# A two-layer graph network on one core: 15 of 1563 gathered chunks fetched row by row by the SyncE queue, with joint register loads and a third buffer for z

## Chip, core and metric

The kernel runs on one core of one Trainium2 chip. A core has TensorE (PE, matrix products, with a separate weight load, PEld), VectorE (DVE), ScalarE (ACT), GpSimd (POOL) and SyncE (SP, which here only issues transfers). The engines run their own instruction streams in order and wait for one another through semaphores. The metric is the device time of one execution in microseconds (us), the median over several runs.

## What is computed

Two message-passing layers over the same graph, with 12,500 nodes of 64 features, 200,000 edges sorted by destination, and 8 edge types. Each layer's result is added to its input and normalised. Cut to what matters:

```python
# layer 1: a message of each edge, summed by destination
all_feat = concatenate([x[dst], x[src], edge_attr, u_per_node[dst]])
msg = relu(all_feat @ W1 + b1)
agg = segment_sum(msg, dst)
x = layernorm(x + relu(concatenate([x, agg, u_per_node]) @ W2 + b2))

# layer 2: attention over the edges of a destination, by edge type
Z = einsum('ni,rio->nro', x, fc_weight)        # (node, type, 64)
z_s, z_d = Z[src, etype], Z[dst, etype]
e = relu(sum(concatenate([z_s, z_d]) * attn_weight[etype], axis=1))
ex = exp(e - segment_max(e, dst)[dst])
alpha = ex / segment_sum(ex, dst)[dst]
x = layernorm(x + segment_sum(alpha * z_s, dst))
```

In the second layer one row of Z is needed for each edge: the row of its source node and its type.

## The kernel before

**Tiling.** Edges come in chunks of 128 (`EC`), one edge per partition. Four chunks make a run (`KS`), which shares one window of 96 (`W`) destinations. Two runs make a group of eight chunks (`K`). There are 1563 chunks and `NG` = 196 groups; the last has three chunks.

**Layer 1** (some 0 to 2600 us) gathers rows of a table from DRAM for each chunk (L95), forms the messages, and sums them by one-hot matrix products. `finish0` turns a tile of 125 nodes into the first layer's output and into that tile's rows of Z, which go through a tile `z` (L477 to L481) to the DRAM table `z_tab`. That has one row for each node and type, with `C` = 65 values (260 bytes): the 64 of Z and the source's share of the score. A smaller table `d_tab` holds the destinations' shares.

**Layer 2** (some 2640 to 5340 us) is `sum1`, one Python generator per group. Its pieces, in order:

- The loads. SP: `row` (L501, four buffers), two registers with the windows' first nodes (L330), and two window loads into `dw` (L600, four buffers) whose DRAM addresses are in those registers. POOL: eight indirect transfers (L95), one for each chunk, each of 128 rows of `z_tab` into `zg` (five buffers).
- `ps_row`, `off`, `ohT`, `pq` (L609 to L618): the destinations' shares, by PE and ACT.
- `oh` (L355): the one-hot matrix, on DVE, in one instruction of 0.95 us.
- `er`, `ed`, `e`, score, `oe` to `t` (L624 to L646): scores and their maximum by destination, on DVE. Score is the first that reads `zg`.
- Transposes (L652), then register loads on DVE and ACT, then `m` (L657) and `rows` (L659).
- `most`, `d`, `top` (L667 to L669): the running maximum of each destination, kept in SBUF, its columns addressed by registers.
- `column`, `mq`, `pm` (L677, L428 to L431, L684): the maximum is brought back to each edge. `pm` is eight small matmuls.
- `em` (L688, L689), the exponentials (L690, L692), and `wz` (L694): eight ACT instructions that scale the rows of `zg`. They are the last that read `zg`, and free it.
- `sums` (L698), sixteen PE matmuls, and `acc` (L702, L703).

`finish1` turns 125 nodes of `acc` into the layer's output (from iteration 90, `FIRST`), with a load of `xn` on SP. `scale1` normalises every fourth iteration, and SP stores four tiles of `out` (L744).

**Order.** The loop runs over `i` from -3 to `NG` - 3. An iteration advances several groups by a piece each, in an order written out by hand in calls of `group()` and `node()`, which the compiler keeps on each engine. The loads of group i+3 come first. SP and POOL have nothing else in their streams, so they run ahead of the other engines as far as the buffers allow. SP issues in order: what waits for a buffer holds back all that is behind it. A transfer with its address in a register is three instructions on SP: register arithmetic, a move and the DMA itself.

**Register loads.** `wins_load` loads each window's number by an instruction of its own, for each of the engines that need it; `group` and `node` are the calls of `next` on the generators.

Of the kernel before, what the change touches and what calls it, by code (L numbers as in the profile page):

```python
# [45 lines left out]
S = 2  # L46
# [7 lines left out]
W = 96  # L54
NWIN = (N + W - 1) // W
GX = 5
FIRST = 90
NSL = NG - FIRST
LAST = 6
# [8 lines left out]


@with_exitstack  # L70
def gnn_kernel(ctx: ExitStack, tc, x, xT, xP, src, dstp, dst, et, eaT, u, W1, b1, W2, b2, fc, aw, out):
    nc = tc.nc
    consts = ctx.enter_context(tc.tile_pool(name="consts", bufs=1))
    keep = ctx.enter_context(tc.tile_pool(name="keep", bufs=1))
# [18 lines left out]
    def gather(to, table, idx, chunks):  # L93
        for k in range(chunks):
            nc.gpsimd.indirect_dma_start(  # L95
                out=to[:, k, :], out_offset=None, in_=table[:, :],
                in_offset=bass.IndirectOffsetOnAxis(ap=idx[:, k:k + 1], axis=0))
        if chunks < to.shape[1]:
            nc.gpsimd.memset(to[:, chunks:, :], 0.0)
# [229 lines left out]
    def window_of(row, at, *engines):  # L329
        return nc.values_load(row[0:1, at], engines=engines, min_val=0, max_val=N - 1,  # L330
                              skip_runtime_bounds_check_because="a destination, so a node")

    def any_left():
        return nc.values_load(rest[0:1, 0:1], min_val=0, max_val=1)

# [97 lines left out]
    def finish0(work, psum, n0_of, dq, xa=xa, i=None, bank="pz"):  # L433

        at = n0_of(ENG.SP)
        xn = work.tile([P, D], F32, name="xn", bufs=6)
        nc.sync.dma_start(xn, x[ds(at, P), :])
        yield
        n0 = n0_of(ENG.DVE)
        yield  # L440
        xs = work.tile([2 * D, P], F32, name="xs")
        nc.vector.tensor_copy(xs, xa[:, ds(n0, P)])
        yield
        po = psum.tile([P, D], F32, name="po")
        nc.tensor.matmul(po, xs, w2x, start=True, stop=True)
        yield
        y = work.tile([P, D], F32, name="y")
        nc.vector.tensor_add(y, po, c2)  # L448
        nc.vector.scalar_tensor_tensor(y, y, 0.0, xn, OP.max, OP.add)
        st = work.tile([P, nc.vector.BN_STATS_DIM], F32, name="ln_st")  # L450
        nc.vector.bn_stats(out=st, in_=y)
        mv = work.tile([P, nc.vector.BN_AGGR_DIM], F32, name="ln_mv")
        nc.vector.bn_aggr(out=mv, in_=st)
        v = work.tile([P, 1], F32, name="ln_v1")
        nc.scalar.activation(v, mv[:, 1:2], AF.Sqrt, bias=eps)
        yield
        nc.vector.reciprocal(v, v)
        x1 = work.tile([P, 2, D], F32, name="x1")
        nc.vector.tensor_scalar(x1, y[:, None, :].to_broadcast([P, 2, D]), mv[:, 0:1], v, OP.subtract, OP.mult)
        nc.sync.dma_start(place("x1", i)[ds(at, P), :], x1[:, 0, :])  # L460
        yield

        pz = psum.tile([128, 2, 512], F32, name=bank)
        px = pz[:, 1, 256:256 + P]
        nc.tensor.transpose(px, x1.rearrange("p h d -> p (h d)"), ident[:P, :P])
        yield
        x1T = work.tile([2 * D, P], F32, name="x1T")
        nc.vector.tensor_copy(x1T, px)
        yield
        for h in range(2):  # L470
            rows = slice(h * D, (h + 1) * D)
            nc.tensor.matmul(pz[:P, h, :256], x1T[rows], fcw[rows, h * NR // 2:(h + 1) * NR // 2, :], start=True, stop=True)
        yield
        pw = psum.tile([P, D], F32, name="pw")
        nc.tensor.matmul(pw[:, :2 * NR], x1T[:D], wsd.rearrange("d s r -> d (s r)"), start=True, stop=True)  # L475
        yield
        z = work.tile([P, NR, D + 1], F32, name="z")  # L477
        nc.scalar.copy(z[:, :, :D].rearrange("p (h r) d -> p h r d", h=2),
                       pz[:P, :, :256].rearrange("p h (r d) -> p h r d", d=D))
        nc.vector.tensor_copy(z[:, :, D], pw[:, :NR])  # L480
        nc.sync.dma_start(  # L481
            place("z", i)[ds(at * NR, P * NR), :].rearrange("(p r) c -> p (r c)", r=NR),
            z.rearrange("p r c -> p (r c)"))
        parts(work, pw[:, NR:2 * NR], lambda i: dq[:, i * NR:(i + 1) * NR], [P, NR])
        nc.sync.dma_start(place("d", i)[ds(at, P), :], dq)
# [6 lines left out]
    def span(g):  # L492

        n = min(S, NRE - g * S)
        return n, min(n * KS, NCE - g * K), slice(g * K, g * K + n * KS)

    def row_load(work, g):
        def load():
            n = span(g)[0]
            row = work.tile([1, n, RE], BF16, name="row", bufs=4)  # L500
            nc.sync.dma_start(row, rel_tab[g * S:g * S + n, :].rearrange("(o s) e -> o s e", o=1))  # L501
            return row
        return load

    def wins_load(g):
        return lambda engine: [window_of(base_row, slice(g * S + s, g * S + s + 1), engine) for s in range(span(g)[0])]

    def all_of(pieces):
        for _ in pieces:
# [13 lines left out]
    def group(g):  # L523
        if 0 <= g < NG:
            next(groups[g], None)

    def node(i):
        if i in slots:
            next(slots[i], None)
# [63 lines left out]
    sums = ctx.enter_context(ExitStack())  # L593
    acc, top = sums_of(sums.enter_context(tc.tile_pool(name="late", bufs=1)))

    def sum1(work, psum, n, chunks, idx, rel_of, et_of, row_of, wins_of, odd=0):
        row = row_of()
        dw = work.tile([W, n, Q], BF16, name="dw", bufs=4)
        for s, b in enumerate(wins_of(ENG.SP)):
            nc.sync.dma_start(dw[:, s, :], d_tab[ds(b, W), :])  # L600
        zg = work.tile([EC, n * KS, C], F32, name="zg", bufs=5)
        gather(zg, z_tab, idx, chunks)
        yield

        off = work.tile([W, n, RE], BF16, name="off")
# [140 lines left out]
    with (  # L746
        tc.tile_pool(name="l1", bufs=2) as work,
        tc.tile_pool(name="l1_ps", bufs=1, space=PSUM) as pool,
        tc.manual_schedule(),
    ):  # L750
        psum = Banks(pool, pq=2, pb=2)
        groups, slots, ys, scales, places = {}, {}, {}, {}, {}

        def y_of(i):
            q, at = divmod(i - FIRST, NQ1)
            if at == 0:
                ys[q] = (work.tile([P, NQ1, D], F32, name="y1"),
                         work.tile([P, NQ1, nc.vector.BN_AGGR_DIM], F32, name="ln_mv"))
            return ys[q][0][:, at, :], ys[q][1][:, at, :]

        for i in range(-3, NG - 2):
            g = i + 3
            if g < NG:
                n, chunks, c = span(g)
                groups[g] = sum1(work, psum, n, chunks, row_i[:, c], rel[:, c], et_i[:, c],
                                 row_load(work, g), wins_load(g), g % 2)
            if i >= FIRST:
                slots[i] = finish1(work, psum, slot(i), lambda i=i: y_of(i), lambda n0, i=i: places.update({i: n0}))
            group(i + 3)
            node(i)  # L770
            group(i)
            group(i - 1)
            group(i + 2)
            group(i + 1)
            group(i + 2)
            node(i - 3)
            group(i)
            group(i)
            group(i + 2)
            group(i - 1)  # L780
            group(i - 1)
            group(i + 1)
            group(i)
            group(i)
            group(i - 1)
            group(i - 2)
            group(i - 1)
            group(i)
            node(i - 3)
            for q in scales:  # L790
                next(scales[q], None)
            group(i)
            node(i - 2)
            for q in scales:
                next(scales[q], None)
            q, at = divmod(i - 3 - FIRST, NQ1)
            if i - 3 >= FIRST and at == NQ1 - 1:
                js = range(i - 3 - at, i - 2)
                scales = {q: scale1(work, [places[j] for j in js], *ys[q], js)}
                next(scales[q])  # L800
        some = any_left()
        for i in (NG - 2, NG - 1):
            slots[i] = finish1(work, psum, slot(i), lambda i=i: y_of(i), lambda n0, i=i: places.update({i: n0}))

        q = (NSL - 1) // NQ1
        first = FIRST + q * NQ1

        def batch(q, js):
            yield from scale1(work, [places[j] for j in js], *ys[q], js, last=True)

        scales = {NG: batch(q - 1, range(first - NQ1, first)), NG + 1: batch(q, range(first, NG))}
        in_order("""
            g-3 g-2 g-3 g-2 g-1 g-3 g-3 g-1 g-2 g-2 g-2 g-4 g-2 g-1 n-2 g-2 g-3 g-1 g-2 g-2 n-5 g-1 g-2 g-1
            g-1 n-4 n-5 g-2 n-4 g-1 g-3 n-4 g-1 g-1 n-3 g-1 g-2 g-1 g-2 n-2 g-1 n-3 n-3 n-1 s0 n-2 n-2 g-1
            g-1 n-1 n-1 s0 s0 n-1 s1 s1 s1""")
# [92 lines left out]
```

## Time and profile before

| | |
|---|---|
| median of 13 runs (5323.22 to 5354.6 us) | 5344.73 us |
| the profiled execution | 5342.42 us |
| its span | 5340.6 us |
| PE busy | 2956.4 us (55%) |
| POOL busy | 2961.8 us (55%) |
| DVE busy | 2486.8 us (47%) |
| ACT busy | 1443.8 us (27%) |
| gathers of `zg` on POOL, 1563 | 1478.3 us, 946 ns each |
| `wz` on ACT (L694), 1564 | 394.7 us, 335 ns each |
| POOL busy in 2700 to 3000 us | 169.57 us of 300 |
| POOL busy in 4500 to 4800 us | 160.80 us of 300 |
| granted TensorE clock | 0.549 |

The profile is of one execution. A group of equal instructions is given as line, engine, operation, output and inputs, with its busy time and the mean of one; behind the bar stands the time its engine was idle before them, and what ended most of that. In the timeline a row is start, duration, engine, line, operation and tile; square brackets give the idle time before it and its releaser. "Remote" or "another core or an unknown queue" is a release that the records do not explain; with one core it is no other core. The ends of matmuls are modelled. "SPq", "DVEq" and the like are the engine's sequencer, which handles registers and issues transfers; its work is not counted as busy.

### The profile page before, as it was taken

How to read it: one execution, taken by the hardware profiler on the slowest of the kernel's cores; microseconds unless marked ns; L12 is line 12 of the kernel's file. 1: busy time of each engine (PE TensorE's matmuls, PEld its weight loads, DVE VectorE, ACT ScalarE, POOL GpSimd, SP SyncE). 2: the span in 40 equal slices, each digit the busy share in tenths (PEclk: the TensorE clock that was granted, in tenths of full speed). 3: DMA queues.
4: the chain of work that ended last, by engine and by line, in shares of the span. 5: the costliest groups of instructions: out<-in, count | busy, mean ns of one | idle time of the engine just before them, and what ended most of it. 6: DMA issues, size and time to landing. Idle time of an engine off the chain costs nothing.

```text
span 5340.6 us, 63566 instructions
## 1 busy us (share of the span) xinstructions
PE 2956.4 (55%) x16633; PEld 2306.2 (43%) x16634; DVE 2486.8 (47%) x8113; ACT 1443.8 (27%) x3717; POOL 2961.8 (55%) x3140
## 2 busy tenths in 40 slices
PE   3455555555777777777444545445545454454454
PEld 2344444444555555556333333333333333333333
DVE  2022222222444444445455555555556566556566
ACT  1000000000111111111333433433344444454444
POOL 5466665665656656654355555555555555555553
PEclk6555555555556556566655555555555555555555
DMA  3121111111222222222111111111111111111111
GB/s 123 30 62 37 37 36 36 36 36 37 57 62 64 64 61 64 64 61 67 40 22 21 21 22 20 22 22 21 21 24 25 26 25 26 26 23 26 25 25 20
DMA packets 294061, 204.93 MB, mean 38 GB/s; under 512 B 214573, under 2 KB 214703, under 8 KB 293274
## 3 DMA queue, kind: packets, MB, share of 16 engines
q0 software_dynamic: 100032, 103.43, 9.7%
q1 hardware_dynamic: 189180, 87.46, 6.4%
q10 hardware_dynamic: 4480, 9.91, 0.6%
q8 instruction: 134, 2.20, 0.2%
q14 instruction: 235, 1.93, 0.1%
HBM read 158.55 MB, written 41.97 MB: 38 GB/s over the span
## 4 chain that ended last, share of the span: by engine, by line
another core or an unknown queue 35%; DVE 22%; PE 16%; issue 14%; ACT 10%; DVEq 2%; DMA 0%; ACTq 0%; POOL 0%; SPq 0%; POOLq 0%
PE pa L416 7%; ACT wz L694 5%; PE pm L401 3%; DVE oh L355 3%; DVE psc L642 2%; DVE oe L642 2%; DVEq L330 1%; DVE d L668 1%; DVE most L667 1%; DVE ed L627 1%; DVE psc L644 1%; DVE t L645 1%; DVE t L646 1%; DVE msg L410 1%
## 5 line engine op out<-in xcount | busy, mean ns | idle before, releaser
L95 POOL DMA_INDIRECT zg<-z_tab,row_i x1563 | 1478.3, 946 | 1308.8 <-ACT top L669 739.6
L95 POOL DMA_INDIRECT bg<-b_tab,src_i x1523 | 1441.8, 947 | 1007.0 <-issue 399.5
L698 PE MATMUL pb<-oh,wz 128*65 128x96 f32 x3128 | 551.7, 369 | 633.0 <-ACT wz L694 451.7
L416 PE MATMUL pa<-oh,msg 128*64 128x96 f32 x3128 | 539.3, 364 | 566.4 <-ACT msg L411 449.2
L698 PEld LDWEIGHTS pb<-oh,wz 128*65 128x65 f32 x3128 | 495.2, 227 | 689.1 <-ACT wz L694 492.8
L416 PEld LDWEIGHTS pa<-oh,msg 128*64 128x64 f32 x3128 | 482.8, 222 | 592.9 <-ACT msg L411 463.3
L411 ACT ACTIVATE msg<-msg 128x512 f32<-128x512 f32 x191 | 120.0, 628 | 2088.5 <-DVE msg L410 1943.6
L401 PEld LDWEIGHTS pm<-aw,cb 128*128 128x128 f32 x3128 | 581.2, 285 | 136.9 <-issue 132.7
L401 PE MATMUL pm<-aw,cb 128*128 128x64 f32 x3128 | 620.7, 377 | 2.3 <-issue 2.3
L422 DVE TENSOR_TENSOR xa<-xa,pa 64x96 f32 x391 | 100.9, 258 | 837.8 <-remote 526.5
L410 DVE TENSOR_TENSOR msg<-pm,bg 128x512 f32<-128x512 f32 x191 | 131.3, 688 | 721.1 <-remote 598.6
L610 ACT ACTIVATE off<-ps_row,minus_p 96x512 bf16<-96x512 f32 x391 | 266.5, 681 | 496.3 <-remote 194.4
L694 ACT ACTIVATE wz<-zg,wz 128x64 f32<-128x64 f32 x1564 | 394.7, 335 | 6.4
L355 DVE TENSOR_TENSOR oh<-psc,rel 128x768 f32<-128x768 f32 x392 | 371.4, 948 | 7.2 <-DMA z_tab<-z 4.3
L609 PE MATMUL ps_row<-row,ones_row 1*96 1x512 bf16 x391 | 220.2, 563 | 275.6 <-ACT off L610 130.4
L659 PE MATMUL pt<-ident,m 96*65 96x96 f32 x782 | 176.3, 379 | 353.8 <-issue 140.4
L688 DVE TENSOR_REDUCE em<-pb 128x8 f32<-128x24 f32 x196 | 35.4, 181 | 595.7 <-remote 544.8
L690 ACT ACTIVATE pb<-d 65x192 f32<-65x192 f32 x196 | 64.4, 328 | 823.7 <-DVE em L688 482.3
L659 PEld LDWEIGHTS pt<-ident,m 96*65 96x65 f32 x782 | 119.5, 219 | 371.2 <-issue 145.4
L396 DVE TENSOR_SCALAR cb<-ps_row,iota_p 96x1024 f32<-96x1024 f32 x196 | 246.2, 1256 | 11.0 <-issue 9.4
L475 PE MATMUL pw<-wsd,x1T 64*125 64x16 f32 x212 | 60.7, 364 | 312.2 <-DVE y L448 311.6
L475 PEld LDWEIGHTS pw<-wsd,x1T 64*125 64x125 f32 x212 | 50.7, 295 | 374.0 <-DVE y L448 373.1
(151 smaller groups left out, 3993.0 us busy)
## 6 DMA issues: line engine op xcount, KB each, us to landing
z_tab<-z SPq DMA_DIRECT2D x106, 253.9 KB
zg<-z_tab,row_i POOLq DMA_INDIRECT x1563
cb<-in_eaT SPq DMA_DIRECT2D x195, 128.0 KB
bg<-b_tab,src_i POOLq DMA_INDIRECT x1523
aw<-a_tab SPq DMA_DIRECT2D x391, 24.0 KB
dw<-d_tab SPq DMA_DIRECT2D x391, 4.7 KB
row<-rel_tab SPq DMA_DIRECT2D x390, 2.0 KB
xn<-in_x SPq DMA_DIRECT2D x106, 31.2 KB
```

The source lines that it names most:

```text
L95: nc.gpsimd.indirect_dma_start(out=to[:, k, :], out_offset=None, in_=table[:, :], in_offset=bass.IndirectOffsetOnAxis(ap=idx[:, k:k + 1], ...
L355: nc.vector.tensor_tensor(oh, iota_n[:, None, :].to_broadcast([EC, n * KS, W]), rel_of.unsqueeze(2).to_broadcast([EC, n * KS, W]), OP.is_e ...
L396: nc.vector.tensor_scalar(cb[:W, :, :], ps_row, iota_p[:W], None, OP.is_equal)
L401: nc.tensor.matmul(pm[:, k, :], cb[:, s, i * EC:(i + 1) * EC], aw_t[:, s, :], start=True, stop=not raw)
L410: nc.vector.tensor_add(msg, pm, bg)
L416: nc.tensor.matmul(pa[D:, s, :], msg[:, k, :], oh[:, k, :], start=(i == 0), stop=(i == KS - 1))
L609: nc.tensor.matmul(ps_row[:, :RE], ones_row, row[:, s, :], start=True, stop=True)
L610: nc.scalar.activation(off[:, s, :], ps_row[:, :RE], AF.Abs, bias=minus_p[:W])
L642: nc.vector.tensor_mul(to, by_run[:, :, i, :], es[:, :, i].unsqueeze(3).to_broadcast([EC, n, half, W]))
L659: nc.tensor.matmul(rows[:, s, :], m[:, s:s + 1].to_broadcast([W, C]), ident[:W, :W], start=True, stop=True)
L694: nc.scalar.activation(wz[:, k, :D], zg[:, k, :D], AF.Copy, scale=wz[:, k, D:])
L698: nc.tensor.matmul(sums[:, s, :], wz[:, k, :], oh[:, k, :], start=(i == 0), stop=(i == KS - 1))
```

## The change

Three things change.

- For 15 groups (18, 30, ..., 186) the last of the eight chunks is no longer gathered by POOL. SP fetches its 128 rows one by one, 260 bytes each, into a buffer `zo` with the size of `zg` (one buffer). Each row's address comes from a register. Thirteen rows are fetched in each of ten iterations, 10 to 1 before the group's loads (the last has eleven); so of every twelve iterations ten fetch. Before each thirteen, one instruction loads thirteen registers. The addresses, (source × 8 + type) × 65, are worked out by two DVE operations on one partition, from two rows of indices that SP loads one iteration earlier. POOL gathers the other seven chunks into the same `zo`, and such a group takes no `zg` buffer.
- The two window numbers of a group are loaded into registers by one instruction for each engine that needs them, in both layers, and not by two. In all 240 fewer register loads on SP (the thirteens counted against them), 390 fewer on DVE and 195 fewer on ACT.
- `z` in `finish0` has three buffers, not two.

In numbers of instructions: SP gets 1,950 more DMAs and 1,920 more of register arithmetic, POOL 15 fewer gathers, DVE 30 more operations. PE is the same. Two inputs, `srcr` and `etr`, hold the padded source and type of the edges as one row per chunk.

```diff
+OWN = range(18, NG - 6, 12)
+AHEAD, PER_SP = 10, 13
...
+    def values(row, engine, most):
+
+        return list(nc.values_load_multi_w_load_instructions(
+            row, engines=[engine], min_val=0, max_val=most,
+            skip_runtime_bounds_check_because="each is of a node")[1])
...
-        z = work.tile([P, NR, D + 1], F32, name="z")
+        z = work.tile([P, NR, D + 1], F32, name="z", bufs=3)
...
     def wins_load(g):
-        return lambda engine: [window_of(base_row, slice(g * S + s, g * S + s + 1), engine) for s in range(span(g)[0])]
+        return lambda engine: values(base_row[0:1, g * S:g * S + span(g)[0]], engine, N - 1)
...
-    def sum1(work, psum, n, chunks, idx, rel_of, et_of, row_of, wins_of, odd=0):
+    def sum1(work, psum, n, chunks, idx, rel_of, et_of, row_of, wins_of, odd=0, zg=None):
...
-        zg = work.tile([EC, n * KS, C], F32, name="zg", bufs=5)
-        gather(zg, z_tab, idx, chunks)
+        if zg is None:
+            zg = work.tile([EC, n * KS, C], F32, name="zg", bufs=5)
+            gather(zg, z_tab, idx, chunks)
+        else:
+            gather(zg[:, :chunks - 1, :], z_tab, idx, chunks - 1)
         yield
...
+        waiting, fetched = [], {}
+        z_row = z_tab.rearrange("n c -> (n c)")
+
+        def fetch(engine, name, n):
+
+            if waiting:
+                g, at, own_i = waiting[0]
+                n = min(n, EC - at)
+                places = values(own_i[0:1, at:at + n], name, (N * NR - 1) * C)
+                for p, b in enumerate(places, at):
+                    engine.dma_start(fetched[g][p:p + 1, K - 1, :], z_row[ds(b, C)].rearrange("(o d) -> o d", o=1))
+                waiting[:1] = [(g, at + n, own_i)] if at + n < EC else []
...
+            if i + AHEAD + 1 in OWN:
+                own_i, own_t = (work.tile([1, EC], I32, name=name) for name in ("own_i", "own_t"))
+                for t, a in ((own_i, srcr), (own_t, etr)):
+                    nc.sync.dma_start(t, a[:, (i + AHEAD + 1) * K + K - 1, :])
+            if i + AHEAD in OWN:
+                g = i + AHEAD
+                nc.vector.scalar_tensor_tensor(own_i, own_i, float(NR), own_t, OP.mult, OP.add)
+                nc.vector.tensor_scalar_mul(own_i, own_i, float(C))
+                fetched[g] = work.tile([EC, K, C], F32, name="zo", bufs=1)
+                waiting.append((g, 0, own_i))
             group(i + 3)
+            fetch(nc.sync, ENG.SP, PER_SP)
             node(i)
```

The gather, which stays as it is, and which the edit calls with seven chunks:

```python
    def gather(to, table, idx, chunks):
        for k in range(chunks):
            nc.gpsimd.indirect_dma_start(
                out=to[:, k, :], out_offset=None, in_=table[:, :],
                in_offset=bass.IndirectOffsetOnAxis(ap=idx[:, k:k + 1], axis=0))
        if chunks < to.shape[1]:
            nc.gpsimd.memset(to[:, chunks:, :], 0.0)
```

More of the change, by code (lines that the diff above doesn't have):

```diff
@@ L70, in gnn_kernel @@
 @with_exitstack
-def gnn_kernel(ctx: ExitStack, tc, x, xT, xP, src, dstp, dst, et, eaT, u, W1, b1, W2, b2, fc, aw, out):
+def gnn_kernel(ctx: ExitStack, tc, x, xT, xP, src, srcr, dstp, dst, et, etr, eaT, u, W1, b1, W2, b2, fc, aw, out):
     nc = tc.nc
@@ L765, in gnn_kernel @@
                 groups[g] = sum1(work, psum, n, chunks, row_i[:, c], rel[:, c], et_i[:, c],
-                                 row_load(work, g), wins_load(g), g % 2)
+                                 row_load(work, g), wins_load(g), g % 2, fetched.get(g))
             if i >= FIRST:
                 slots[i] = finish1(work, psum, slot(i), lambda i=i: y_of(i), lambda n0, i=i: places.update({i: n0}))
+            if i + AHEAD + 1 in OWN:
[8 more added lines that the diff above has]
+                waiting.append((g, 0, own_i))
             group(i + 3)
+            fetch(nc.sync, ENG.SP, PER_SP)
             node(i)
@@ L884 @@
         "src": by_chunk[0],
+        "srcr": srcp.reshape(1, NC, EC),
         "dstp": by_chunk[1],
@@ L887 @@
         "et": by_chunk[2],
+        "etr": etp.reshape(1, NC, EC),
         "eaT": eap.reshape(NRUN, RE, DE).transpose(0, 2, 1),
```

## The prediction

> **What bounds the kernel now.** First the share of each engine, then the chain that ended last.
>
> ```profile
> PE 2956.4 (55%) x16633; PEld 2306.2 (43%) x16634; DVE 2486.8 (47%) x8113; ACT 1443.8 (27%) x3717; POOL 2961.8 (55%) x3140
> ...
> another core or an unknown queue 35%; DVE 22%; PE 16%; issue 14%; ACT 10%; DVEq 2%; DMA 0%; ACTq 0%; POOL 0%; SPq 0%; POOLq 0%
> ...
> L95 POOL DMA_INDIRECT zg<-z_tab,row_i x1563 | 1478.3, 946 | 1308.8 <-ACT top L669 739.6
> ```
>
> No engine is full. POOL, whose gathers the change thins out, waits as long as it works, and a third of the chain has no owner. So I took the waits of 2800 to 4800 us, inside the second layer (engine, its line, the releaser; total us, times, longest):
>
> ```profile
> POOL zg L95 <- ACT top L669: 547.5, 125, 9.2
> DVE em L688 <- remote: 435.0, 109, 5.4
> ```
>
> The first is POOL waiting for a zg buffer: the loop holds POOL, not POOL the loop. The second is the ownerless time: em waits 435.0/109 = 4.0 us for the eight small matmuls pm (L684). The timeline tells why. One iteration between gathers, then one in the tail, where no gather runs:
>
> ```profile
> 3802.41 0.35 PE L684 MATMUL pb<-mq,ohT 96*128 96x3 bf16 x8
> ...
> 3803.73 0.95 POOL L95 DMA_INDIRECT zg<-z_tab,row_i  x1 [0.30 <-issue]
> 3804.98 0.95 POOL L95 DMA_INDIRECT zg<-z_tab,row_i  x1 [0.30 <-issue]
> 3806.23 0.94 POOL L95 DMA_INDIRECT zg<-z_tab,row_i  x1 [0.30 <-issue]
> ...
> 3808.20 0.18 DVE L688 TENSOR_REDUCE em<-pb 128x8 f32<-128x24 f32 x1 [4.64 <-remote]
> ...
> 3811.20 0.94 POOL L95 DMA_INDIRECT zg<-z_tab,row_i  x1 [4.03 <-ACT top L669]
> ...
> 5292.05 0.35 PE L684 MATMUL pb<-mq,ohT 96*128 96x3 bf16 x8 [0.16 <-DVE mq L431]
> ...
> 5293.11 0.17 DVE L688 TENSOR_REDUCE em<-pb 128x8 f32<-128x24 f32 x1
> ```
>
> pm to em takes 5.79 us beside gathers and 1.06 us without. So while a run of gathers goes on, PE takes a step only every 5.79/8 = 0.72 us; the modelled busy times hide it. From the times at which DVE and SP resume around such runs I read that this sets in 2 to 3 us after a run's start and lasts until some 1.8 us past its end. A run of eight is 7×1.25+0.95 = 9.70 us, so about 9.0 us (9.70 - 2.5 + 1.8) of each period are slow. A period, from one run's start to the next's, is 13.4 us before the node pieces join at iteration 90 and 13.8 us after.
>
> SP is held back in the same stretches. Pairs of window loads (line DMA x2: start, us from the first's start to the second's end), in the first layer beside gathers, then in the second between two runs:
>
> ```profile
> 1507.47 2.12 SPq L384 DMA_DIRECT2D aw<-a_tab  x2
> ...
> 3813.72 0.99 SPq L600 DMA_DIRECT2D dw<-d_tab  x2
> ```
>
> From one DMA's start to the next's that is 1.42 us (the second itself shows 0.70) against 0.52 us (0.47). Each needs register work and a DMA, just what a fetch of a row needs. I take 1.45 us slow, 0.52 us fast, a factor of 2.8.
>
> **The change, part by part.**
>
> *Removed from POOL:* 15 gathers × (0.95+0.30) = 18.75 us. POOL waits, so this is no time saved by itself: each run shortens by 1.25 us, and so does the slow stretch, in which the loop goes at about half its rate (9 us of it hold some 4.7 us that the tail does not have). I take 0.6 us × 15 = -9 us; ends 0 and -18.75. An own group also takes no zg buffer, so POOL can run one group ahead. That joins two runs and leaves a gap later. The slow stretch moves and shrinks by no more than the gather removed: nothing, within the same ends.
>
> *Joint loads:* 390 fewer on DVE, 195 on ACT, 240 fewer on SP net. The trace has them (us as ns, min/median/max):
>
> ```profile
> L330 SPq TENSOR_LOAD <-base_row x782: 2/416/1430, 87.8 to 5272.7; - x196
> L330 DVEq TENSOR_LOAD <-base_row x782: 297/302/550, 97.4 to 5317.1; - x196
> ```
>
> DVE's stand behind oh (L355, 0.95 us) ahead of m, which waits for transposes, and ACT's ahead of em's wait: hidden, 0. Without cover they would be 390×0.30 = 117 us on DVE. If a load of two registers costs two loads, nothing is lost. *Third z buffer:* a layer-1 ACT copy waits for an older store; the period there (12.5 us) is a gather run and its tail, so 0. If it were the bound, the gain is below 1 us of each 12.5 and I give it no term. *DVE's addresses:* 2 operations on one partition × 128, nearest row 0.2 us (a small tensor op such as L624's 0.21), ×15 = +6 us on DVE's chain.
>
> *Added on SP:* 1,920 single-row fetches, 150 register loads of 13 (or 11), 30 index loads. SP issues in order: what waits behind a fetch is row and dw of a later group, then x and out, and the row's consumers (ps_row, off, ohT, pq) hang on it. They are issued three iterations ahead, and the index arithmetic on DVE stops SP once in twelve iterations, taking about one of the three. So SP's mean over twelve iterations decides. In fast time:
>
> - base: row 0.3, joint load 0.5, two dw 2×0.52: 1.9 us. With nodes +1.5 (a slot load 0.4, xn 0.5, one out 0.55).
> - ten of twelve iterations: a load of 13 plus 12.8×0.52 = 6.7 us. Mean with own loads (0.6 per twelve): (10×(1.9+0.5+6.7)+2×1.9+0.6)/12 = 7.9 us; with nodes 9.4.
>
> The load of 13 is not shown. Low end: one instruction at the cost of one register, 0.27 us (ACT's loads of the same line). High end: 13×0.27 = 3.5 us. I take 0.5, since the nearest row is one load, 0.42 median. A period P offers (P-9.0)+9.0/2.8 = P-5.8. So P = 13.7 without and 15.2 with nodes, against 13.4 and 13.8. The 15 blocks of twelve iterations fill iterations 8 to 187: 82 without nodes, 98 with. 82×0.3 = +25 and 98×1.4 = +137. At present SP idles about 9 us of a period, which looks like room for 13×0.52 = 6.8 us; most of those 9 us lie in the slow stretch, where they hold a third of that.
>
> The Trainium skill ("Runtime: NRT & Kernel Launch", Instruction fetch mechanics) speaks against this part: a register load costs about 200 ns a register even in bulk. The DVE row, 302 ns for one, fits neither side. By the rule an estimate of 2.6 us for 13 adds 1.75 us to SP's mean and 180×1.75 = 315 us to the sum.
>
> *Waits.* Each SP DMA waits for the one eight back: 8×0.52 = 4.2 us, twice that slow, and the nearest landing, a gather's, lies within the 1.8 us past a run's end; so 0. If rows landed later than 4.2 us, SP would lose the rest of each fast stretch; bounded by the slow price everywhere, below. The first fetch of a group waits for wz of the last own group (one zo buffer), two iterations earlier in the order: 0, since SP is stopped by DVE there anyway.
>
> *Sum,* against the profiled execution, 5342.4 us: -9 +6 +25 +137 = +159, 5501 us. It stands 2.3 us below the median of 5344.7, so **5504 us**.
>
> *Ends.* Load at 0.27: -0.19×180 = -34. At 3.5: +2.5×180 = +450. Slow fetch 1.35 us (a pair a little quicker than the quoted one): 9/2.6 instead of 9/2.8, -45. At 2.1 us: factor 4, +0.95×180 = +171. No node extra on SP: -137. So from +0 to about +780 if all add up.
>
> **Rivals.**
>
> *SP's room is enough (faster).* For it: about 9 us idle in each period (in the timeline, SP's register work for dw ends at 3804.6 and its DMA goes at 3813.72); rows are due only when their group is summed; a fetch may be less hindered than a pair with window loads. It decides if a slow fetch costs below 1.05 us (factor 2: 9/2+4.4 = 8.9, near 9.4). Then only -9+6 remains, down to -18.75 and some hidden waits: 5323 to 5342, 5330 as its time. Against it: the 1.42 us above, and in those stretches PE is slow as well, which no queue of SP explains.
>
> *The load counts each register and the slow fetch costs 2.1 us (much slower).* +159+450+171 = 5342+780, 6120 us at the worst; half of the two, 5800 and above. For it: SP loads up to 1.43 us in the row above. Against: median 0.42.
>
> *The gain is eaten (no change).* SP just copes; -9 from POOL meets +6 on DVE: 5342. For it: POOL's idle time. It needs the same room as the first.
>
> *SP's traffic slows PE.* If PE and SP share what the gathers hold up, 1,920 fetches each delay a matmul by one 0.7 us step where pm is waited for; on the stretch of 5.8 of 13.6 us: 1,920×0.43×0.7 = +570 us at most, 5900. Against it: pm is just as slow in periods where SP issues nothing during the wait.
>
> **How the numbers follow.** "The same" is within 0.2% (11 us), about what a measurement of this kernel can tell. The forecast, 5360 to 5800: 0.45. Above 5800 by load price or PE: 0.11. Slower for less, 5356 to 5360: 0.02. Faster: 0.35. Same: 0.07. Together faster 0.35, same 0.07, slower 0.58. The likeliest case has 5360 to 5800; as its complement is mostly the faster case, the range reaches down to 5318 and up to 5800, leaving out 0.11 above and about 0.04 below.
>
> **What would show it.** Right: SP's DMAs for zo in steps of about 1.4 us during a run of gathers and 0.5 us after it; mean periods near 13.7 and 15.2 us between iterations 8 and 187; new waits of PE's ps_row on row (L501) or pq on dw. POOL's idle time grows. Wrong: the periods stay or fall and SP still idles in the loaded iterations (factor too high); the 13-register load is long (load price); em's wait grows past 4.0 us (PE's step). If layer 1, up to 2600 us, moves by more than 5 us, the zero for the z buffer was wrong.

## The result, and the profile after

The changed kernel takes 5632.79 us (median of 8 runs, 5614.36 to 5649.85) against 5345.69 us before: a ratio of 1.0534, 95% interval 1.0523 to 1.0545, or +287 us. The profiled execution has a span of 5623.7 us. The forecast was slower, 5504 us in 5318 to 5800; that range reaches from 27 us below the time before to 455 us above it, so that a time inside it says little by itself.

The first lines of the page, and the gathers of `zg` (line numbers have moved: L97 was L95, L337 was L330, L620 was L609, L643 was L632, L699 was L688):

```profile
PE 2944.3 (52%) x16633; PEld 2301.9 (41%) x16634; DVE 2486.1 (44%) x8143; ACT 1444.3 (26%) x3717; POOL 2946.9 (52%) x3125
...
L97 POOL DMA_INDIRECT zg<-z_tab,row_i x1443 | 1364.8, 946 | 1580.7 <-ACT top L680 1081.4
```

Every engine is busy for about as long as before, PE 12 us and POOL 15 us less. The whole loss is idle time: POOL's ahead of `zg` went from 1308.8 to 1580.7 us. So something that is not counted as busy became late.

When did it happen? `em` comes once a group. From group 12's to group 84's (before the nodes) the starts are 2817.2 and 3794.5 us before, 2815.0 and 3900.4 after: 977.3 against 1085.4 us, +108. From there to group 192's, at 5302.0 and 5585.7: 1507.5 against 1685.3 us, +178. What lies ahead of group 12 changed by -2.2 us. The mean period went from 13.6 to 15.1 us without nodes and from 14.0 to 15.6 with them. Within a block of twelve, most periods are 14.5 us, two or three are 17 to 24 us, and one or two are 9 to 12 us.

The long ones have an owner. The groups of DVE instructions that add the gathered score to `e`, which is the first to read `zg` or `zo` (behind the bar: busy and mean; idle before and what ended it). Before:

```profile
L632 DVE TENSOR_TENSOR e<-e,zg 128x8 f32<-128x8 f32 x196 | 33.9, 173 | 11.6 <-DVE e L630 2.0 <-issue 0.6
```

After, the 15 own groups stand apart from the others:

```profile
L643 DVE TENSOR_TENSOR e<-e,zg 128x8 f32<-128x8 f32 (+1 forms) x181 | 31.1, 172 | 10.2 <-DVE e L641 1.6 <-issue 0.2
L643 DVE TENSOR_TENSOR e<-e,zo 128x8 f32<-128x8 f32 x15 | 2.6, 172 | 178.7 <-DMA xn<-x_tab 71.3 <-DMA zo<-z_tab 51.4 <-DMA row<-rel_tab 23.6
```

DVE stood idle 178.7/15 = 11.9 us before each own group's `e`. The named releasers are guesses between transfers that ended together. In 14 of the 15 groups this `e` starts 0.9 to 2.9 us after SP issued the group's last fetched row. The rows themselves came late. Six of these waits, 64.1 us together, lie before the nodes. The timeline around group 150 (SP's transfers and two DVE instructions):

```profile
4906.85 0.17 DVE L699 TENSOR_REDUCE em<-pb 128x8 f32<-128x24 f32 x1
...
4918.66 6.10 SPq L774 DMA_DIRECT2D zo<-z_tab  x11
...
4926.01 0.17 DVE L643 TENSOR_TENSOR e<-e,zo 128x8 f32<-128x8 f32 x1 [14.45 <-DMA xn<-x_tab]
...
4930.52 0.17 DVE L699 TENSOR_REDUCE em<-pb 128x8 f32<-128x24 f32 x1
```

The last eleven rows go out just when DVE should use them; DVE waits 14.45 us, and this period is 23.7 us. The second victim is PE's `ps_row`, which needs `row` from the same queue:

```profile
L620 PE MATMUL ps_row<-row,ones_row 1*96 1x512 bf16 x391 | 216.6, 554 | 393.7 <-issue 146.7 <-ACT off L621 96.8 <-DMA row<-rel_tab 82.4
```

Before, its idle time was 275.6 us, and `row` was not among the releasers named. Of the 82.4 us, 74.4 lie between groups 84 and 192 and none between groups 12 and 84: before the nodes `row` was issued a median of 16.0 us ahead of the `ps_row` that reads it, and it came in time.

Where SP's time goes, from the instructions of the register loads (ns, min/median/max) and one loaded iteration of the timeline:

```profile
L337 SPq TENSOR_LOAD <-base_row x392: 2/676/1917, 86.9 to 5556.1; - x196
L337 DVEq TENSOR_LOAD <-base_row x392: 300/532/780, 97.9 to 5600.7; - x196
L337 SPq TENSOR_LOAD <-own_i x150: 3/2263/2687, 2732.1 to 5488.0; - x150
```

```profile
4794.13 0.52 SPq L608 DMA_DIRECT2D dw<-d_tab  x2
4797.55 12.58 SPq L774 DMA_DIRECT2D zo<-z_tab  x13
4810.96 0.31 SPq L721 DMA_DIRECT2D xn<-x_tab  x1
4811.37 0.23 SPq L509 DMA_DIRECT2D row<-rel_tab  x1
```

The 2.9 us between the end of `dw` and the first row of `zo` are the load of thirteen registers and the first row's register work. The thirteen rows take 12.58 us beside gathers. From the next `dw` pair on it begins again: a loaded iteration has no pause of 9 us any more. Most of what is left of SP's idle time is one stop in twelve iterations, where it waits for the index arithmetic on DVE (129.4 us in 12 waits between 2800 and 5100 us). Over the whole trace, successive rows stand 1.43 us apart in the median where both lie in a stretch that gathers slow (2.5 us after a run's start to 1.8 us past its end; 606 intervals), and 0.39 us where both lie outside (1007).

### The profile page after: what moved, and what is told of

It is laid out like the page before. It is cut to its first block, busy times and chain, and to the rows that moved or that the text cites. A ratio compares the mean times of both kernels' runs of the same rounds, so it can differ in the third digit from the quotient of the medians.

```text
span 5623.7 us, 68800 instructions
## 1 busy us (share of the span) xinstructions
PE 2944.3 (52%) x16633; PEld 2301.9 (41%) x16634; DVE 2486.1 (44%) x8143; ACT 1444.3 (26%) x3717; POOL 2946.9 (52%) x3125
## 5 line engine op out<-in xcount | busy, mean ns | idle before, releaser
L97 POOL DMA_INDIRECT zg<-z_tab,row_i x1443 | 1364.8, 946 | 1580.7 <-ACT top L680 1081.4
L97 POOL DMA_INDIRECT bg<-b_tab,src_i x1523 | 1441.9, 947 | 1001.4 <-issue 399.8
L620 PE MATMUL ps_row<-row,ones_row 1*96 1x512 bf16 x391 | 216.6, 554 | 393.7 <-issue 146.7
L705 ACT ACTIVATE wz<-zg,wz 128x64 f32<-128x64 f32 x1444 | 364.4, 335 | 5.9
L668 DVE TENSOR_REDUCE m<-pt 96x2 f32<-96x256 f32 x196 | 81.7, 417 | 507.1 <-remote 356.4
L663 PE MATMUL pt<-ident,t 128*96 128x128 f32 x391 | 119.2, 406 | 287.7 <-DVE mq L436 229.7
L404 DVE TENSOR_SCALAR cb<-ps_row,iota_p 96x1024 f32<-96x1024 f32 x196 | 246.2, 1256 | 12.4 <-issue 9.4
L663 PEld LDWEIGHTS pt<-ident,t 128*96 128x96 f32 x391 | 55.2, 193 | 427.5 <-issue 361.5
```

Source lines behind the costliest of these rows:

```text
L97: nc.gpsimd.indirect_dma_start(out=to[:, k, :], out_offset=None, in_=table[:, :], in_offset=bass.IndirectOffsetOnAxis(ap=idx[:, k:k + 1], ...
L404: nc.vector.tensor_scalar(cb[:W, :, :], ps_row, iota_p[:W], None, OP.is_equal)
L620: nc.tensor.matmul(ps_row[:, :RE], ones_row, row[:, s, :], start=True, stop=True)
L663: nc.tensor.transpose(tt[:, s, :], t[:, s, :], ident[:EC, :EC])
L705: nc.scalar.activation(wz[:, k, :D], zg[:, k, :D], AF.Copy, scale=wz[:, k, D:])
```

## The experiments

The three sets ran on three chips, and there the kernel before takes 3963 to 3971 us, not 5345; each comparison is therefore with before on the same chip, as a ratio. The record doesn't name the chip of the first profile. That it was a fourth one is taken from the times, not shown; "the first chip" stands for it. The difference that matters here is seen in the trace of the first experiment (second layer, nodes on):

```profile
3303.12 0.35 PE L695 MATMUL pb<-mq,ohT 96*128 96x3 bf16 x8
3303.19 0.94 POOL L97 DMA_INDIRECT zg<-z_tab,row_i  x1 [0.30 <-issue]
...
3304.19 0.17 DVE L699 TENSOR_REDUCE em<-pb 128x8 f32<-128x24 f32 x1
3304.44 0.94 POOL L97 DMA_INDIRECT zg<-z_tab,row_i  x1 [0.30 <-issue]
```

In the middle of gathers, which take the same 0.94 us at the same rhythm, the eight small matmuls are done in 1.07 us. PE and SP do not go in steps on these chips. (The granted TensorE clock is higher too, 0.59 against 0.55, but at 0.55 the same eight matmuls took 1.06 us where no gather ran.) Then POOL is the bound, eight gathers a period without a gap: 8×1.25 = 10.0 us, the period measured. So the experiments test what the added work on SP does where no steps occur; what the steps add on the first chip is read from its two traces alone.

**Only the two small edits.**

```diff
-OWN = range(18, NG - 6, 12)
+OWN = ()
```

> Leaves out the row fetches (all groups gathered by POOL); keeps the joint loads and z's third buffer. Theory (SP's time for the fetches is the whole loss, the two small edits are hidden): 5335 to 5355 us, within 0.2% of before. Rival (the small edits give or cost something that the fetches hide): outside that, for instance 390 x 0.3 = 117 us less if DVE's loads were on the path, or more if a joint load costs more than two.

Measured: 3963.70 us, ratio 1.0001 (0.9992 to 1.001). Joint loads and the third buffer give nothing and cost nothing. That agrees with the first chip, where the time ahead of group 12 changed by 2.2 us. The joint load is hardly cheaper than two: 532 ns on DVE for two registers, above, against 302 ns for one.

**The fetches into a tile that nobody reads.**

```diff
-        else:
-            gather(zg[:, :chunks - 1, :], z_tab, idx, chunks - 1)
...
-                                 row_load(work, g), wins_load(g), g % 2, fetched.get(g))
+                                 row_load(work, g), wins_load(g), g % 2)
```

> Fetches as in the change, but into a spare tile that nobody reads; POOL gathers all eight chunks of every group into zg. Theory (SP has no time): the rows of a group can no longer be late for DVE, but row and dw still stand behind the fetches; SP's mean need of 8.3 us (9.8 with nodes), with the load of 13 at the measured 2.67 us, gives periods of 14.1 and 15.6 us, 5560 to 5630 us. Rival 1 (the loss is from own groups taking no zg buffer, so that runs of gathers join): these joins are gone, so below 5430 us. Rival 2 (the fetches slow PE's steps): 5600 us or more, with em's wait above 4 us in ordinary periods.

Measured: 4068.81 us, ratio 1.0265 (1.0249 to 1.0281), +106 us, less than the theory's 1.040 to 1.053, which was worked out for the first chip with its steps. The waits of 3000 to 3900 us (L617 is `ps_row` here; total us, times, longest):

```profile
PE ps_row L617 <- DMA row<-rel_tab: 213.2, 53, 10.2
```

With no join of gather runs and no DVE reading `zo`, the loss comes through `row`. Periods stay at 10.0 us without nodes and are 11.1 us with them (groups 12 to 84, and 96 to 190). PE is not slower (a median of 1.28 us from the start of `mq`'s last operation to `em`, as in the others), so on this chip neither rival holds.

**One transfer in place of 128 fetches.**

```diff
-                places = values(own_i[0:1, at:at + n], name, (N * NR - 1) * C)
-                for p, b in enumerate(places, at):
-                    engine.dma_start(fetched[g][p:p + 1, K - 1, :], z_row[ds(b, C)].rearrange("(o d) -> o d", o=1))
+                if at == 0:
+                    engine.dma_start(fetched[g][:, K - 1, :], z_tab[g * EC:(g + 1) * EC, :])
```

> The 128 fetches and ten register loads of a group are replaced by one transfer of 128 rows at a fixed place (other rows than the reference's); POOL still gathers seven chunks into zo without a zg buffer. Theory: SP has its room again, 5325 to 5350 us. Rival 1 (joined runs of gathers): about 5 us a block stays, 15 x 5 = +75, 5400 to 5440 us. Rival 2 (fetches slow PE): as the theory.

Measured: 3943.75 us, ratio 0.9952 (0.9937 to 0.9967), -19.4 us. That is 15 gathers × 1.25 = 18.75 us, the whole of what POOL was spared, since POOL is the bound there. Own groups without a `zg` buffer cost nothing on this chip. Whether joined runs cost something where PE steps is not told by it.

**Fetching two iterations earlier.**

```diff
-OWN = range(18, NG - 6, 12)
-AHEAD, PER_SP = 10, 13
+OWN = range(18, NG - 6, 14)
+AHEAD, PER_SP = 12, 13
```

> Fetches of 13 groups instead of 15, every fourteenth group, starting twelve instead of ten iterations ahead: the rows are due two iterations after the last is issued. Theory: DVE no longer waits for the last row (about 10 us a group), and SP's mean need over fourteen iterations falls to 7.4 us (8.9 with nodes): periods 13.4 and 14.7 us, 5400 to 5470 us. Rivals 1 and 2: 13/15 of the loss stays, 287 x 13/15 = +249, about 5595 us.

Measured: 4040.65 us, ratio 1.0194 (1.0178 to 1.021), against 13/15 of the whole change's loss on such a chip, 1.0255 (next experiment). In its waits of 3000 to 3900 us:

```profile
PE ps_row L620 <- DMA row<-rel_tab: 199.5, 48, 10.2
...
DVE e L643 <- DMA zg<-z_tab,row_i: 3.4, 6, 1.1
```

DVE no longer waits for own rows, but the wait has moved to `row`: the rows' deadline alone is not the trouble, the queue's time is. And the mean over the pattern is not the whole of it. With nodes SP's instructions and the waits between its `out` stores (next experiment) come to 9.9 us an iteration, just under the 10.0 on offer, and yet the period is 10.9. A loaded iteration takes 12.4 us on average, ten follow one another, and the lead that `row` has before them, 19 us at most, doesn't last through 10×2.4 us.

**The changed kernel on such a chip.** No edit.

> The changed kernel itself, unchanged, beside before on the chip of this set. On the chip of the last set before takes 3963 us, its periods are 10.0 us and neither SP nor PE goes in steps during gathers. If this set runs there too: theory (SP's time): SP's mean need of 8.3 us without nodes fits into 10.0 and of 9.8 us just fits, but the last rows are due one iteration after their issue, so nothing to +3% (3960 to 4080 us), all of it after iteration 90. If it runs on a chip like that of the first profile: +5.0 to 5.6%. Rivals (joined runs of gathers, PE slowed by the fetches): a loss without nodes too.

Measured: 4078.88 us, ratio 1.0294 (1.0277 to 1.0311), +116 us. All of it comes after iteration 90, as the theory had it: periods are 9.9 us without nodes and 11.3 us with them (the same groups as above). Register loads and SP's timeline, undisturbed by steps:

```profile
L337 SPq TENSOR_LOAD <-base_row x392: 526/731/2217, 55.4 to 4018.5; - x196
L337 SPq TENSOR_LOAD <-own_i x150: 980/2672/2703, 2073.0 to 3961.6; - x150
```

```profile
3253.67 0.31 SPq L721 DMA_DIRECT2D xn<-x_tab  x1
3254.07 0.23 SPq L509 DMA_DIRECT2D row<-rel_tab  x1
3255.34 0.85 SPq L608 DMA_DIRECT2D dw<-d_tab  x2
3259.11 5.46 SPq L774 DMA_DIRECT2D zo<-z_tab  x13
3265.41 0.30 SPq L721 DMA_DIRECT2D xn<-x_tab  x1
```

From `xn` to the next `xn` SP needs 3265.41 - 3253.67 = 11.74 us without any pause, in a period of 10.0 us. Of these 2.70 are the load of thirteen (2.67 in the median) and 5.46 the rows, 0.39 apart in the median. Every fourth iteration has more, the four stores of `out`:

```profile
3185.15 0.30 SPq L721 DMA_DIRECT2D xn<-x_tab  x1
3186.38 5.58 SPq L755 DMA_DIRECT2D out<-y  x4
3192.06 0.24 SPq L509 DMA_DIRECT2D row<-rel_tab  x1
```

Each store waits until the one before it has landed, so that they are 1.7 us apart in the median, and `row` stands behind them. SP's own waits show it (2800 us to the end):

```profile
SPq L755 <- DMA out<-y: 97.5, 75, 1.7
```

Counted from one `row` to the next between groups 96 and 190, SP takes 12.65 us in a loaded iteration on average (17.2 with the stores, 10.8 without) and 3.4 in the two light ones, 11.1 us over twelve. That is the period of 11.3 us but for the stop at the index arithmetic. Without nodes it is 9.75 and 2.6, or 8.6 over twelve, and there is no loss.

**Loads without fetches, and fetches without loads.**

```diff
                 places = values(own_i[0:1, at:at + n], name, (N * NR - 1) * C)
-                for p, b in enumerate(places, at):
-                    engine.dma_start(fetched[g][p:p + 1, K - 1, :], z_row[ds(b, C)].rearrange("(o d) -> o d", o=1))
+                if at == 0:
+                    engine.dma_start(fetched[g][:, K - 1, :], z_tab[g * EC:(g + 1) * EC, :])
```

> Keeps the 150 register loads of 13 and drops the 128 fetches of a group for one transfer of 128 rows at a fixed place (other rows than the reference's). Theory: SP's loaded iteration needs 1.9 + 2.7 = 4.6 us (6.1 with nodes), which fits: the loss is gone, within 0.5% of before. Rival (the loads by themselves hold SP back): a loss above 1%.

```diff
-                places = values(own_i[0:1, at:at + n], name, (N * NR - 1) * C)
-                for p, b in enumerate(places, at):
-                    engine.dma_start(fetched[g][p:p + 1, K - 1, :], z_row[ds(b, C)].rearrange("(o d) -> o d", o=1))
+                for p in range(at, at + n):
+                    engine.dma_start(fetched[g][p:p + 1, K - 1, :], z_tab[g * EC + p:g * EC + p + 1, :])
```

> The 1,920 fetches of one row each stay, but from fixed addresses, so without register loads and register arithmetic (other rows than the reference's). Theory: SP's need in a loaded iteration falls from 9.6 us by the load of 2.67 us and by some 0.1 us a row, to about 5.7 us (7.2 with nodes); on a chip without steps the loss is gone, on one with steps one instruction a row in place of three takes at least 0.7 us beside gathers, and a third of the loss or less stays (5345 to 5440 us). Rival (it is the number of DMAs, each waiting for the one eight back): the loss stays whole.

Measured: 3945.36 us, 0.9958 (0.9944 to 0.9972), and 3946.10 us, 0.9958 (0.9941 to 0.9974). Each alone keeps nearly the whole gain. Neither the number of transfers, with their waits for the one eight back, nor the loads cost anything by themselves on such a chip: only their sum exceeds the period.

**Half as many, thinner.**

```diff
-OWN = range(18, NG - 6, 12)
-AHEAD, PER_SP = 10, 13
+OWN = range(30, NG - 6, 24)
+AHEAD, PER_SP = 22, 6
```

> Seven own groups instead of 15, every twenty-fourth, six rows an iteration in 22 iterations. Theory: SP's need in a loaded iteration is 1.9 + 1.3 + 6 x 0.4 = 5.6 us (7.1 with nodes): it fits, no row is late, and the gain is 7 gathers, -9 us at most: 0.995 to 1.002 of before. Rivals (joined runs, PE slowed): 7/15 of the loss of the changed kernel on the same chip.

Measured: 3953.89 us, 0.9978 (0.9969 to 0.9988), -8.8 us: seven gathers × 1.25 = 8.75 us.

**One load for ten iterations.** A direct test of the term that the prediction had to guess; rows after the first thirteen are the wrong ones here.

```diff
-                places = values(own_i[0:1, at:at + n], name, (N * NR - 1) * C)
-                for p, b in enumerate(places, at):
+                if at == 0:
+                    held[:] = values(own_i[0:1, at:at + n], name, (N * NR - 1) * C)
+                for p, b in enumerate(held[:n], at):
```

> The changed kernel with one register load of 13 a group instead of ten; the ten fetches of an iteration go on from the same 13 registers (other rows than the reference's, many of them again and again). All 1,920 fetches, their register arithmetic and the seven-chunk gathers stay. Theory (SP's time, in which the load of 13 at 2.67 us is the term sized wrongly): on a chip like that of the last two sets SP's mean need falls by 9 x 2.67 / 12 = 2.0 us to about 9.5 with nodes, below the period of 10.0: the loss is gone, 0.995 to 1.003 of before. On a chip like that of the first profile it falls from about 10.6 to 8.6 with nodes and from 9.2 to 7.2 without, against the 8.0 and 7.6 on offer: +0.5 to +2% instead of +5.3%. Rival (the fetches, not the loads, are too much): at least half of the loss stays.

Measured: 3952.27 us, 0.9953 (0.9938 to 0.9969). The loss is gone with all 1,920 fetches, and the `out` stores, in place. In its waits of 3000 to 3900 us:

```profile
PE ps_row L620 <- DMA row<-rel_tab: 20.5, 15, 3.2
...
DVE e L643 <- DMA zo<-z_tab: 11.9, 3, 5.6
```

The wait for `row` is a seventh of the changed kernel's 150.7 us in the same stretch of its own trace.

**A version that beats both.** Thirteen rows an iteration before the nodes, six after.

```diff
-OWN = range(18, NG - 6, 12)
-AHEAD, PER_SP = 10, 13
+OWN = {**{g: (10, 13) for g in range(18, 80, 12)}, **{g: (22, 6) for g in range(102, NG - 6, 24)}}
```

> Ten own groups: six with 13 rows an iteration (18 to 78, before the nodes), four with six rows an iteration in 22 iterations (102 to 174). Correct rows. Theory: on a chip like that of the last two sets SP has the time in both stretches, so the whole of 10 x 1.25 = 12.5 us is gained, 0.996 to 0.9975 of before. On a chip like that of the first profile the dense part costs what it does in the changed kernel without nodes (+108 us in seven blocks, so some +90 in six), the thin part nothing: 1.013 to 1.020.

Measured: 3957.58 us, 0.9967 (0.9955 to 0.9979): faster than before, and than the changed kernel's 1.0294 in the set before. Ten gathers × 1.25 = 12.5 us were expected and 13.5 measured. On the first chip neither this nor the thin version was run.

## Why the prediction was right, and where it was not

**Direction held, and the mechanism with nodes.** SP's time per iteration was named as what decides, with the 9 idle us lying where they hold little. On the chips without steps SP's time and the period can be laid side by side: 11.1 us against 10.0 on offer with nodes, where the loss is, and 8.6 without, where there is none. On the first chip the loaded iteration has no pause either. But +25 us were forecast there without nodes and +137 with, and +108 and +178 came, from periods of 13.6 and 14.0 us before (the prediction read 13.4 and 13.8).

**The step that failed is the price of the register load.** It was taken at 0.5 us, "since the nearest row is one load", with 3.5 us as the upper end. It is 2.67 us, 13 × 0.205. The nearest row was the nearest in kind, not in size: the work is per register, as two registers already show (0.53 us on DVE against 0.30 for one). The Trainium skill's 200 ns a register ("Runtime: NRT & Kernel Launch", Instruction fetch mechanics), set beside it and not taken, fits this row within 3%. It fits the load of one on DVE less well, at 302 ns. The one-load run shows that this term is enough to make the difference between gain and loss on the chips without steps.

**A second term was too small, the nodes' extra.** It was put at 1.5 us an iteration, with one `out` at 0.55. On the chip without steps it is 2.5 (11.1 less 8.6), since each of the four stores waits for the landing of the last: 1.7 us apiece. How much of the loss would go with these waits alone was not tested.

**Two other prices.** A row fetched outside slow stretches costs 0.39 us, not 0.52: its DMA instruction takes 0.23 us where that of a window load takes 0.33, while the register work is the same to 0.01 us. The slow one, 1.43 us, was right at 1.45.

**The formula for what a period offers fits with nodes and fails without.** The load is not slowed like the rows: on the first chip 39 of the 150 loads lie in slow stretches, and from the last `dw` to the first row there it is 2.9 us at most. A period of P then offers P-4.5 (of the 9.0 us, 2.7 at face value and 6.3/3.5). As an estimate with SP's 8.6 and 11.1 us, P is 13.1 and 15.6. The second is the 15.6 us measured. The first is less than the 13.6 us before, so SP's mean gives no loss without nodes, where 15.1 us and +108 us were measured. There, as shown above, nothing waited for `row`, which the prediction had named; DVE waited 64.1 us for own rows, and the ordinary period of 14.5 us was longer by the time that `em` waits (below). So in this part the side was right partly by luck: SP's slow fetches cost time, but through a wait that the prediction had put at nothing.

**What is late next** was named as `row` and its consumers. With nodes they are, but on the first chip the fetched rows themselves come first: 178.7 us of DVE's idle time, against 82.4 us of PE's for `row`. "Rows are due only when their group is summed" was put under the faster rival; it is a deadline one iteration after the last fetch. On the first chip it was missed even before the nodes, where by the estimate above SP keeps up in the mean.

**The rival that SP's traffic slows PE has a part.** On the first chip the time from the start of `mq`'s last operation to `em` has a median of 6.0 us before and 6.8 us after. It is 6.8 us, too, in the 31 ordinary loaded periods without nodes, which are 14.5 us long against 13.5 before. Already before, in the 36 groups in which SP issued twelve or more instructions in that time, its median was 6.8 us, and 5.3 us in the 55 in which SP issued none; so the prediction's "just as slow in periods where SP issues nothing" was misread. That is about one more step of 0.7 us. At some 0.8 us × the 150 loaded iterations it would be 120 us at most, some 50 of them before the nodes, where 64 and 50 come near the +108. This is read from traces, not tested: no experiment ran on such a chip. Nor were joined runs of gathers, whose long periods (24.4, then 9.4 us) are among the rest.

**What held:** the zeros for the joint loads and `z` (ratio 1.0001); nearly no wait of a row for the transfer eight back (fetches without loads: no loss; in the trace after, SP's waits of that kind between rows of `zo` sum to 31.2 us in 2800 to 5100 us). The gain of -9 us for the gathers could not be measured on the first chip; on the others it was the full 16.6 to 19.4 us, because there POOL is the bound.

## What to carry to other kernels

An idle queue engine is room only for as many instructions as it can issue there: count them, price a register load by its registers, count the waits of stores for one another, and compare the mean over the whole pattern with the period, not with the idle time. The mean must fit, and it is not enough: what is due right after a burst can still come late. Moving work off the engine that paces a loop paid by the full amount removed (7, 10 and 15 gathers gave 8.8, 13.5 and 19.4 us) where the receiving queue kept up, and turned into a loss where it didn't. So find the dose: half as many rows an iteration, for half as many groups, made a loss of 2.9% a gain of 0.2%. The Trainium skill says that issuing from several engines saves only the sequencer's time, usually small beside the transfer ("DMA: Bandwidth & Descriptors", Issuing engines are not separate DMA queues). For rows of 260 bytes the sequencer's time, 0.39 us a row and 0.2 us for its register, was what decided here.

## What the hardware showed that was not expected

The same program takes 5345 us in the first runs, and 3963, 3963 and 3971 us in the three sets on three other chips (other as far as the times tell). Gathers last the same there (0.945 us). In the first runs alone PE and SP take a step only every 0.7 us while POOL's gathers run. DVE and ACT don't: a joint register load on DVE has a median of 532 ns and one `wz` on ACT takes 335 ns in both. So these steps are no property of the program, and a profile can't tell from itself that another run won't be without them. What makes them is open.

A register load of thirteen takes 2.67 us on SP, of two 0.53 us on DVE and 0.73 us on SP, of one 0.30 us on DVE (medians).
